# A recurrence's products with x in half-blocks of four steps with a fixed order, and the first chunk's gates moved into its head

## The chip, the core and the metric

One core of a Trainium2 chip runs the whole program. The metric is the time of one execution in device microseconds, given as the median of several runs; a profile is one execution. The engines are named as in the profile: PE (TensorE; PEld are its weight loads), DVE (VectorE), ACT (ScalarE), POOL (GpSimd), SP (SyncE, which here issues most DMAs). They run side by side, each works its own queue in order, and they wait for each other by semaphores.

## What is computed

Input x is 64 sequences of 64 steps of 256 numbers (4096 tokens), cond is 64 x 256. The program is a chain of two layers with residual sums. Each has a conditioning, an attention-like part, a second conditioning and a feed-forward part. Two pieces of layer 1 matter here:

```python
# conditioning: a plain recurrence; h starts from cond
xW = x @ Wx + b
h[t] = tanh(h[t-1] @ Wh + xW[:, t])            # Wh, Wx: 256 x 256

# "attention": a state-space block on h, inner width 512, 16 states
xi, z = split(h @ W_in)                        # 512 and 512
xc = silu(conv4(xi) + b_conv)                  # causal, 4 taps
delta_lr, B, C = split(xc @ W_xproj)           # 16, 16, 16
delta = softplus(delta_lr @ W_dt + b_dt)
s[t] = exp(delta * A) * s[t-1] + delta * B * xc
y = (sum over states of s * C + D * xc) * silu(z) @ W_out
```

Around them stand, in order of time: a conditioned scan and attention, a quantized feed-forward part (layer 0), then these two, then two mixtures of experts.

## The kernel before

All of it is float32 unless a line says otherwise. Feature rows lie on the 128 partitions, so 256 features are two halves, k = 0 and 1 (or o = 0 and 1 on the output side); tokens lie along the free axis. A framework schedules the instructions of each engine from the program text: it keeps data dependences, gives each a semaphore wait, and may move instructions past each other. An *issue order token* on an instruction pins its place among the instructions with the same token.

**Recurrence** (`rnn`, lines 711 to 756). PSUM tiles of 8 steps x 64 sequences hold what goes into tanh, one bank for each output half: tag `ps` for o = 0, tag `acc` for o = 1, four buffers each. Such a pair is a block; there are eight. First the products with x, xW, are put into the block (`ahead`, line 718): 8 "pieces" of 256 columns each, a piece being 32 sequences x 8 steps for one o and one k. Then, for each step, four products with Wh (line 745; two k, two o, 64 columns each) are added, and two tanh on ACT (line 754) write the new state into `hs`. A step needs the tanh of the step before. After each step one piece of the *next* block is asked for (line 755). Order is up to the scheduler, which can move pieces ahead of where they stand in the text.

In the profile every fp32 product shows as two weight loads and two matmuls.

**State-space stage** (`mamba`, lines 787 to 1052). The 4096 tokens are cut into 8 chunks of 512. `head(c, v)` (line 834) makes a chunk's inputs: four products with W_in (line 844, two matrix products each), which ACT (line 848) and DVE (line 851, three instructions) turn into the convolution; one Silu over the 512 rows (line 855); the product with W_xproj (line 859); softplus in pieces on PE, ACT, DVE and POOL (lines 883 to 897). `gates(c, v, i0)` (line 900) makes silu(z) for half of the rows: two products with W_in (line 906), two copies (line 909), a Silu (line 912). Both are generators that yield after each piece, so that they can be spread over a loop.

The loop (line 995) runs 32 steps a chunk, 256 in all. A step takes two scans on DVE (line 1009) and one product with C (line 1011), with the decay exp(delta A) from ACT (line 977), delta B xc from POOL (line 970), C spread over partitions by PE (line 922, tile `cb`), and eight transposes on PE that sum over the states (line 1025). The next chunk's head and this chunk's gates are queued in `pieces` (line 1001) and taken at a fixed rate, 40 for 30 steps (line 1041); what is left is run two steps before the chunk's end (line 1013).

Chunk 0 has no loop before it, so its head runs alone, ahead of the loop (line 984). Its gates are the first entries of `pieces`. Exp and Silu need different tables on ACT, and a change of table is a load (`ACT_TABLE_LOAD`).

PSUM tiles for single products come from `one()`, which in the first head goes round four tags (line 813) and afterwards always takes `mp` (line 986).

## Time and profile before

| | us |
|---|---|
| median of 10 runs | 2877.03 (2873.50 to 2880.23) |
| the profiled execution | 2877.23 |
| its span, first to last instruction | 2875.2 |
| recurrence, first Wh product to last tanh | 638.8 to 738.3 |
| head of chunk 0, to the first scan | 738.3 to 786.5 |
| chunk 0 of the state loop, nearly | 786.5 to 905 |

The page gives shares of the span in which each engine is busy: PE 84%, DVE 61%, ACT 49%, POOL 45%. They are means over stages with different limits and say little about one stage. The mean granted clock of TensorE is 0.917 of full speed. How to read the rows that follow: a timeline row has the start and duration in us, the engine, the line of the kernel, the operation, the tile it writes `<-` the tiles it reads, the shape and how many instructions are merged; `[1.31 <-ACT dA L977]` says that the engine stood idle for 1.31 us before it and which instruction ended that.

### The profile page before, as it was taken

To read this page: it belongs to the slowest core of one execution; us is meant where nothing else is said; L and a number is where in the kernel's file an instruction comes from. 1 tells how busy PE (TensorE), PEld (TensorE's weight loads), DVE (VectorE), ACT (ScalarE), POOL (GpSimd) and SP (SyncE) were. 2 spreads that over 40 slices of the span, in tenths; PEclk is the share of its full clock that TensorE was granted. 3 is DMA by queue.
4 is the path that set the end of the run, shared out by engine and by line. 5 is a ranking of instruction groups with operands and counts; after the bars stand their busy time and mean duration, and the time that the engine had idled before them with its cause. 6 is when DMAs were issued, how large, how long until landed. Compare 5 with 4: busy or idle time off the path is not lost.

```text
span 2875.2 us, 34770 instructions
## 1 busy us (share of the span) xinstructions
PE 2406.7 (84%) x12148; PEld 1701.0 (59%) x12148; DVE 1754.0 (61%) x2955; ACT 1412.6 (49%) x2406; POOL 1305.8 (45%) x1117
## 2 busy tenths in 40 slices
PE   4989977779666878888787888868987899999995
PEld 4633334458334555555455555556875778888885
DVE  0567648870299989898987888894244443323322
ACT  0567557764556676767475757643333222222220
POOL 0023335440178676767477777773745351111110
PEclk9979987889576989999899999989999999999998
DMA  9999700010121212121212121222686856555555
GB/s 237 370 358 341 231 25 19 19 63 5 33 71 67 79 64 71 59 82 56 70 63 92 63 96 67 90 80 89 223 288 228 313 192 251 221 187 205 210 189 183
DMA packets 183076, 406.06 MB, mean 141 GB/s; under 512 B 25312, under 2 KB 89056, under 8 KB 177520
## 3 DMA queue, kind: packets, MB, share of 16 engines
q1 hardware_dynamic: 169456, 366.80, 38.0%
q0 software_dynamic: 13440, 36.98, 3.3%
q8 instruction: 98, 1.61, 0.2%
q14 instruction: 82, 0.67, 0.1%
HBM read 280.76 MB, written 144.98 MB: 148 GB/s over the span
## 4 chain that ended last, share of the span: by engine, by line
PE 44%; DVE 20%; ACT 9%; issue 7%; POOL 4%; DMA 3%; SPq 0%; DVEq 0%; POOLq 0%; ACTq 0%
DVE hb L1009 12%; PE ps L1603 11%; PE acc L1501 8%; DVE hb L1011 3%; PE yp L1025 2%; PE ps L1570 2%; PE mq L1739 2%; PE mp L906 2%; PE mq L1755 2%; DVE xc L851 1%; PE ps L628 1%; PE ps L745 1%; POOL hb L970 1%; PE acc L745 1%; PE ps L1611 1%
## 5 line engine op out<-in xcount | busy, mean ns | idle before, releaser
L970 POOL TENSOR_TENSOR hb<-dx,Bn 128x1024 f32<-128x1024 f32 x256 | 601.1, 2358 | 259.0 <-PE yp L1025 252.6
L1009 DVE TENSOR_TENSOR_SCAN hb<-dA,hb 128x512 f32<-128x512 f32 x512 | 603.0, 1209 | 34.6 <-ACT dA L977 32.1
L977 ACT ACTIVATE dA<-delta,A 128x504 f32<-128x504 f32 x512 | 344.5, 683 | 309.3 <-DVE hb L1009 306.7
L1025 PEld LDWEIGHTS yp<-ident,hb 128*128 128x128 f32 x2048 | 267.1, 151 | 184.2 <-issue 146.1
L1011 DVE TENSOR_TENSOR hb<-hb,cb 128x1024 f32<-128x1024 f32 x256 | 312.2, 1220 | 79.2 <-PE cb L922 61.9
L1603 PE MATMUL ps<-gxT,w 128*128 128x256 f32 (+1 forms) x1600 | 323.7, 361 | 0.8 <-DVE gxT L1478 0.8
L1603 PEld LDWEIGHTS ps<-gxT,w 128*128 128x128 f32 x1600 | 276.5, 190 | 46.1 <-issue 11.6
L1025 PE MATMUL yp<-ident,hb 128*128 128x128 f32 x2048 | 301.5, 291 | 0.0
L1739 PE MATMUL mq<-x,moe_s 128*128 128x256 f32 x896 | 251.5, 413 | 48.3 <-ACT up L1746 26.8
L1277 POOL DMA_INDIRECT ffn_y<-gy,to x72 | 69.2, 961 | 432.2 <-ACT gy L1503 420.0
L1739 PEld LDWEIGHTS mq<-x,moe_s 128*128 128x128 f32 x896 | 170.0, 205 | 113.7 <-ACT up L1746 35.8
L1607 DVE TENSOR_TENSOR gh<-gs,ps 128x256 f32<-128x256 f32 (+1 forms) x200 | 78.7, 394 | 207.8 <-ACT gs L1606 207.6
L922 PE MATMUL cb<-parts,pick 80*128 80x512 bf16 x256 | 105.0, 410 | 115.3 <-DVE hb L1011 100.2
L1501 PE MATMUL acc<-w,gh 128*128 128x256 f32 (+1 forms) x864 | 187.4, 387 | 0.0
L1606 ACT ACTIVATE gs<-ps 128x256 f32<-128x256 f32 (+1 forms) x200 | 72.4, 362 | 231.3 <-PE ps L1603 225.4
L1503 ACT ACTIVATE gy<-acc,wt 128x256 f32<-128x256 f32 x152 | 67.0, 472 | 239.3 <-PE acc L1501 231.5
L1501 PEld LDWEIGHTS acc<-w,gh 128*128 128x128 f32 (+1 forms) x864 | 145.7, 189 | 30.6 <-issue 13.8
L426 POOL TENSOR_TENSOR E<-E,z 128x1024 f32<-128x1024 f32 x32 | 61.6, 1925 | 199.4 <-DVE z L425 121.6
L1755 PE MATMUL mq<-moe_s,sh 128*128 128x256 f32 x448 | 115.4, 396 | 6.2 <-ACT up L1746 6.2
L444 PE MATMUL out<-oT,M 128*128 128x512 f32 x256 | 117.9, 604 | 1.5 <-ACT oT L437 1.5
L1277 POOL DMA_INDIRECT moe_y<-gy,to x80 | 78.3, 978 | 79.9 <-ACT gy L1503 54.0
L1755 PEld LDWEIGHTS mq<-moe_s,sh 128*128 128x128 f32 x448 | 83.1, 195 | 41.9 <-issue 20.3
(462 smaller groups left out, 4463.7 us busy)
## 6 DMA issues: line engine op xcount, KB each, us to landing
w<-ffn_w SPq DMA_DIRECT2D x40, 2176.0 KB, 9.3
Bn<-B SPq DMA_DIRECT2D x128, 512.0 KB, 3.6
moe_x<-fill SPq DMA_DIRECT2D x130, 260.0 KB, 5.8
ffn_x<-fill SPq DMA_DIRECT2D x129, 260.0 KB, 6.0
w<-moe_w SPq DMA_DIRECT2D x48, 512.0 KB, 4.5
ffn_w<-in_ffn_W_dram SPq DMA_DIRECT2D x16, 640.0 KB, 8.5
gx<-moe_x SPq DMA_DIRECT2D x32, 260.0 KB, 4.9
gx<-ffn_x SPq DMA_DIRECT2D x32, 260.0 KB, 9.3
```

The lines of the kernel that those rows point to most:

```text
L444: nc.tensor.matmul(ps, M[:, o, ts(k, P)], v.o[:, o], start=(o == 0), stop=(o == H // 2 - 1))
L922: nc.tensor.matmul(t, pick[:, n : n + 1].to_broadcast([rows, P]), v.parts, start=True, stop=True)
L970: nc.gpsimd.tensor_mul(hb, vs[c].dx[p], Bn[:, n % NB, :].unsqueeze(1).to_broadcast([P, PI, CH]))
L977: nc.scalar.activation(decays[s][i][:, :, 1:], seq(vs[c].delta[p][:, i, :])[:, :, 1:], AF.Exp, scale=w.A[:, p * PI + i, n : n + 1],)
L1009: ins = nc.vector.tensor_tensor_scan(h, dA[i].rearrange("p b l -> p (b l)"), h, 0.0, ALU.mult, ALU.add)
L1011: ins = nc.vector.tensor_tensor(hb, hb, cb.unsqueeze(1).to_broadcast([P, PI, CH]), ALU.mult)
L1025: nc.tensor.matmul(yp[i][:, t, :], hb[:, i, ts(t, P)], g.ident, start=(n == 0 and t == 0), stop=(n == S - 1 and t == CH // P - 1), is_tran ...
L1277: i = self.g.nc.gpsimd.indirect_dma_start(out=self.y, out_offset=bass.IndirectOffsetOnAxis(ap=to, axis=0), in_=y, in_offset=None)
L1501: nc.tensor.matmul(po[s], h, w, start=(i == 0), stop=(i == n - 1))
L1603: nc.tensor.matmul(ps[:, j, :], v.w12[:, k, ts(j * (full + 1) + i, P)], v.xT[:, k, :], start=(k == 0), stop=(k == KD - 1))
L1739: nc.tensor.matmul(ps[:, i % 2, :], w[:, k, ts(i, P)], xu[:, k, :], start=(k == 0), stop=(k == KD - 1))
L1755: nc.tensor.matmul(ps[:, t, :], h[:, i, ts(t, P)], self.s2[:, i, :], start=(i == 0), stop=(i == NS - 1))
```

## The change

In the recurrence a piece is now all 64 sequences x 4 steps (still 256 columns), and the outer loop of `ahead` is over the two halves of a block, four steps each. Four pieces are made ahead of step 0. From then on one piece is made after each step, for the four steps that begin up to four steps later: in steps 4 to 7 of a block the first half of the next block, in steps 0 to 3 the second half of the same block. The pieces and the Wh products carry one order token, so they stay in the order of the text. Nothing changes in the number and size of the products, the tanh or the tiles.

In the state-space stage, `gates(0, vs[0], 0)`, the first half of chunk 0's gates, runs inside chunk 0's head after the four convolutions and ahead of the Silu. It is dropped from the loop's `pieces` for chunk 0 alone. So the pieces behind it come four places sooner in that chunk.

```diff
+    TG = TB // 2
+    order = lambda ins: g.tc.stamp_issue_order_token(ins.ins, "recurrence")
     def ahead(t0, ps):
-        for o in range(KD):
-            for half in range(2):
+        for half in range(2):
+            for o in range(KD):
                 for k in range(KD):
-                    nc.tensor.matmul(
-                        ps[o].rearrange("p t b -> p b t")[:, ts(half, B // 2), :],
+                    ins = nc.tensor.matmul(
+                        ps[o].rearrange("p t b -> p b t")[:, :, ts(half, TG)],
                         w.Wx[:, k, ts(o, P)],
-                        xv[:, k, ts(half, B // 2), t0 : t0 + TB],
+                        xv[:, k, :, t0 + half * TG : t0 + (half + 1) * TG],
...
+                    order(ins)
                     yield
...
+    blocks = [[bank(g, (P, TB, B), tag=("ps", "acc")[o]) for o in range(KD)] for _ in range(2)]
+    pieces = ahead(0, blocks[0])
+    for _ in islice(pieces, KD * KD):
+        pass
+    for t in range(L):
+        now = blocks[t // TB]
+        if t % TB == TG and t + TG < L:
+            if t + TG >= 2 * TB:
+                blocks.append([bank(g, (P, TB, B), tag=("ps", "acc")[o]) for o in range(KD)])
+            pieces = ahead(t + TG, blocks[(t + TG) // TB])
...
+                order(ins)
+        for o in range(KD):
+            nc.scalar.activation(hs[:, o, :, t], now[o][:, t % TB, :], AF.Tanh, bias=w.b[:, o : o + 1])
+        next(pieces, None)
...
-        for _ in head(0, vs[0]):
+        first = head(0, vs[0])
+        for _ in islice(first, 2 * NI):
+            pass
+        for _ in gates(0, vs[0], 0):
+            pass
+        for _ in first:
             pass
...
-                pieces = chain(pieces, gates(c, now, 0), islice(ahead, 2 * NI + 1), gates(c, now, PI), ahead)
+                pieces = chain(pieces, gates(c, now, 0) if c else (), islice(ahead, 2 * NI + 1), gates(c, now, PI), ahead)
```

## The prediction

> **What bounds the kernel now.** I read the page's engine shares first, then the stretch tables with the granted clock for 600 to 920 us, where the recurrence and the head of the state-space stage lie, then the timeline there. As a whole the kernel is bound stage by stage, and nothing overlaps the recurrence: between 640 and 738 us only TensorE and ACT work. One step, in the timeline:

> ```profile
> 644.33 0.30 PEld L745 LDWEIGHTS ps<-hs,Wh 128*128 128x128 f32 x2 [0.19 <-ACT hs L754]
> 644.38 0.42 PE L745 MATMUL ps<-hs,Wh 128*128 128x64 f32 x2
> ...
> 645.23 0.30 PEld L723 LDWEIGHTS acc<-xT,Wx 128*128 128x128 f32 x2
> 645.30 0.37 ACT L754 ACTIVATE hs<-ps,rb 128x64 f32<-128x64 f32 x1 [0.78 <-PE ps L745]
> 645.31 0.63 PE L723 MATMUL acc<-xT,Wx 128*128 128x256 f32 x2
> 645.52 0.38 ACT L754 ACTIVATE hs<-acc,rb 128x64 f32<-128x64 f32 x1
> ```

> The loop is: Wh products start (644.33), 0.97 later tanh of ps, 0.37 long, 0.05 later the next Wh: 1.39 a step. The second tanh ends 0.23 after the first. The product with x (L723, "a piece") runs beside the tanh and costs nothing. The stretch table (columns: stretch, its length, busy time of PE, PEld, DVE, ACT, POOL, then granted clock) shows what happens when the pieces are used up, at 702.2, 19 steps before the end:

> ```profile
> 690.00:698.99 8.99, 8.99 (x66) 7.73 (x65) 0.00 (x0) 3.94 (x14) 0.00 (x0) 1.00 0.00 0
> ...
> 705.81:709.23 3.42, 2.95 (x23) 2.52 (x22) 0.00 (x0) 1.30 (x5) 0.00 (x0) 1.00 0.02 5
> 709.23:719.47 10.24, 9.87 (x41) 9.00 (x40) 0.00 (x0) 3.79 (x11) 0.00 (x0) 0.50 0.00 0
> ```

> From 709.23 the clock is half, and a step takes 2.03 instead of 1.39:

> ```profile
> 715.18 0.37 ACT L754 ACTIVATE hs<-ps,rb 128x64 f32<-128x64 f32 x1 [1.21 <-PE ps L745]
> ...
> 717.21 0.37 ACT L754 ACTIVATE hs<-ps,rb 128x64 f32<-128x64 f32 x1 [1.21 <-PE ps L745]
> ```

> Fourteen steps are slow: 14 x 0.64 = 9.0 us. The clock comes back at 743.36, so the head's first products (L844, 0.86 apart in place of 0.43) are slow too. Later, in chunk 0 of the state loop, VectorE is the bound (111.5 busy of 118.5 us, 786.5 to 905), and the gates' Silu makes it wait, since ACT loads a table before and after it:

> ```profile
> 800.79 1.22 DVE L1009 TENSOR_TENSOR_SCAN hb<-dA,hb 128x512 f32<-128x512 f32 x1
> 803.32 1.22 DVE L1009 TENSOR_TENSOR_SCAN hb<-dA,hb 128x512 f32<-128x512 f32 x1 [1.31 <-ACT dA L977]
> ```

> **Part 1, the recurrence.** The work is the same: 64 pieces of 256 columns, 256 Wh products. What moves:

> (a) Start. Before, 8 pieces of the first blocks sit in the feed-forward stage, and 4 stand between step 0 and 1. The pieces taken out of that stage free nothing: ACT's copy at 614.02 waits for TensorE and its own queue alike (L658 ends at 613.98), and the last xT still lands at 637.15. Four pieces follow in both kernels, so step 0 starts at 638.83 in both.

> (b) The new wait. In the changed program's order on TensorE, listed with its waits, a piece of steps 0 to 3 of each block of 8 waits for ACT and the first Wh product behind it carries no wait: the piece writes the second half of the bank whose first half tanh is reading, so it starts only after tanh of its bank. Behind it in the queue stand the Wh products of the next step, and tanh waits for those. Two of the four pieces write ps, two acc. In steps 4 to 7 the piece goes to the other block's bank and stays beside tanh: 1.39.
> Price of a waiting piece: four pieces between 637.21 and the Wh product at 639.04 are 1.83, four between 639.88 and 641.66 are 1.78: 0.445 each, 0.05 more after a pause. From that Wh product to tanh are 0.81 to 0.86 (639.04 to 639.85, 641.66 to 642.52). So a ps step is 0.05 + 0.49 + 0.83 + 0.37 = 1.74, an acc step 0.23 more, 1.97. Bounds: 1.72/1.94 (no pause cost) and 1.83/2.06 (0.44 put on top of 1.39).
> (c) Sum: 16 x 1.74 + 16 x 1.97 + 31 x 1.39 = 102.4 us from step 0 to step 63, against 97.0 (638.83 to 735.85): **+5.4** (bounds +4.6 and +8.2). It holds the 9.0 won and 0.9 won at step 0.
> (d) End. Pieces now reach step 59. The last step at full speed takes 1.6 to the head's first product, at half 2.45: **-0.8**. But without pieces steps 60 to 63 are some 6 us long; before, the halving came 6.4 us after the last piece's end (702.84 to 709.23). So the clock may halve around step 63 (0 to +1.3 us), and the head starts at half clock again: I give no gain there, +0.3 for the steps.

> Will the clock hold in steps 0 to 3? Its changes stand on a grid of 3.41 us (709.23, 743.36, 750.19, 760.43, 763.84). I added up, for each grid stretch, the share in which columns were streamed (0.83 ns a column and pass pair, from L844's 512 columns 0.43 apart; weighted by rows used). Of 677 stretches at full clock, the 58 that were followed by half had shares up to 0.36 (one 0.39), those that were not, 0.365 and more (two lower); back to full it goes from about 0.73. A regular step has (8 x 0.053 + 2 x 0.21)/1.39 = 0.61, one without a piece 0.31, the waiting steps 0.49 and 0.43, and the worst stretch of 3.41 (Wh, pause, piece, Wh, pause, around steps 2 and 3) 0.36. So it should just hold.

> [...]

> **Part 2, gates inside the head.** Added to the head: four L906 products (0.86 each at full clock), two copies (0.58), one Silu (1.06); the table it needs is the one that xc's Silu loads anyway. TensorE is free there (from 747.93 to 755.10). In ACT's queue the copies, the load (1.28) and this Silu stand ahead of xc's Silu, which sets the head. Before, that began 14.84 after the first L844 (738.30 to 753.14). After: 12 products = 10.3 at full clock, some 1.9 for the slow start, then 0.2 + 0.58 + 1.28 + 1.06 = 15.3: **+0.5** (bounds -0.5 and +1.5 by how long the slow start is). What is behind (Wxp product, softplus, POOL's four 2.35 up to the first scan) keeps its length; one convolution of chunk 1 (L848, 0.78 on ACT; three L851) now stands in the gap before the first scan, where VectorE waited 2.22 for POOL.
> Removed from chunk 0's loop: the 1.31 above, and three L851 (0.65 each behind a scan, 805.78 to 806.44): **-3.3**. Bounds: -1.5 (only half of it, if another wait follows) and -9 (all idle of VectorE in chunk 0 is 9.2, some of it waits for cb behind half-clock products). The B store of chunk 1 passes one Bn load on SP; a Bn lands in 3.6 us and is asked for two steps ahead, so nothing; if not, one load, 3.6.

> **Sum**, on the profiled execution's 2877.23 (span 2875.2; the median of the ten, 2877.03, is the same): +5.4 - 0.8 + 0.3 + 0.5 - 3.3 = +2.1: **2879 us**, no change that can be told.

> **The rivals.**
> A, forecast: clock holds, 2873 to 2885. Chance 0.58.
> B, **slower: the clock halves within the recurrence.** Place: the pauses of 0.4 and 0.65 in steps 2 and 3. It decides at a share of about 0.36; mine is 0.36, and with acc steps of 2.06 it would be 0.33. At half clock a step with a piece is TensorE-bound, 4 x 0.42 + 0.86 = 2.54, share 0.67, below the 0.73 that brings the clock back, so it stays. A block then costs 4 x 1.15 + 2 x 1.18 + 2 x 1.37 = 9.7 more. From the middle on, 39 us: 2918; from the first block 78; only in the last, 2888. Against it: 0.42 to 0.45 in other stages held. 0.27.
> C, **faster by the loop**: VectorE's 9.2 us of waiting in chunk 0 go with the gates: 2879 - 8 = 2871. For: cb waits of 0.99 and 1.28 behind half-clock products. Against: L844 and the other gates remain. 0.10.
> D, the wait of (b) doesn't bite: 16 x 0.35 + 16 x 0.58 = 14.9 less: 2864. Against: the queue is in order. 0.05.

> **How the numbers follow.** 0.2% (5.8 us) is about what can be told from no change. Same: 0.42 of A, 0.05 of C: 0.47. Slower: 0.12 of A, all of B: 0.39. Faster: 0.04 of A, half of C, D: 0.14. The range leaves out most of C and D and B's early half: 2872 to 2915; A's own is 2873 to 2885.

> **What would show it.** Right: tanh-to-tanh spacing in a block 1.74, 1.74, 1.97, 1.97, then four of 1.39; granted clock 1.00 up to step 60; the step without piece gone but for the last four; xc's Silu directly behind the gates' Silu; no table load at the fifth scan. Wrong: clock 0.50 inside the recurrence (B), waiting pieces that start with tanh (D), or chunk 0 shorter by more than 5 us (C).

## The result and the profile after

| | kernel before | changed kernel |
|---|---|---|
| median, same chip | 2876.66 us (28 runs, 2870.25 to 2880.38) | 2890.55 us (8 runs, 2887.12 to 2897.12) |
| ratio, 95% interval | | 1.0052 [1.0043, 1.0061] |
| profiled execution, its span | 2877.23, 2875.2 | 2891.60, 2889.4 |

The change makes the kernel 0.5% slower. The forecast was 2879 with a range of 2872 to 2915. The time lies inside that range, but outside forecast A's own 2873 to 2885, and what happened is rival B. By stages of the two profiled spans:

| stage | before | after | difference |
|---|---|---|---|
| up to the first tanh | 639.9 | 640.8 | +0.9 |
| recurrence, first tanh to end of the last | 98.4 | 127.2 | **+28.8** |
| head of chunk 0, to the first scan | 48.2 | 46.8 | -1.4 |
| chunk 0 of the state loop | 131.1 | 124.5 | **-6.6** |
| chunks 1 to 7, to the last scan | 1034.3 | 1027.9 | -6.4 |
| mixtures, to the end | 923.3 | 922.2 | -1.1 |
| span | 2875.2 | 2889.4 | +14.2 |

**The waiting steps.** The timeline of the changed kernel, block 0, where the prediction showed the step of 1.39 us (L757 is tanh, L726 the piece, L752 the Wh products):

```profile
642.60 0.37 ACT L757 ACTIVATE hs<-ps,rb 128x64 f32<-128x64 f32 x1 [1.23 <-PE ps L752]
...
644.42 0.37 ACT L757 ACTIVATE hs<-ps,rb 128x64 f32<-128x64 f32 x1 [1.23 <-PE ps L752]
644.64 0.37 ACT L757 ACTIVATE hs<-acc,rb 128x64 f32<-128x64 f32 x1
...
645.06 0.70 PE L726 MATMUL acc<-xT,Wx 128*128 128x256 f32 x2 [0.46 <-ACT hs L757]
...
645.59 0.38 PE L752 MATMUL ps<-hs,Wh 128*128 128x64 f32 x2
...
646.45 0.37 ACT L757 ACTIVATE hs<-ps,rb 128x64 f32<-128x64 f32 x1 [1.45 <-PE ps L752]
...
648.49 0.37 ACT L757 ACTIVATE hs<-ps,rb 128x64 f32<-128x64 f32 x1 [1.45 <-PE ps L752]
...
649.88 0.37 ACT L757 ACTIVATE hs<-ps,rb 128x64 f32<-128x64 f32 x1 [0.79 <-PE ps L752]
```

Follow one acc step. The tanh of acc ends at 644.64 + 0.37 = 645.01. Only then, at 645.06, does the piece for acc start, and the bracket names tanh as what it waited for. The next Wh product stands behind it in the queue and starts at 645.59, though both halves of the state that it reads were written by then; the next tanh starts at 646.45. The spacing of the first tanh of each step in this block is 1.82, 1.82, 2.04, 2.04, then 1.39 four times. The step without a wait is the last row: 649.88 - 648.49 = 1.39.

**The clock.** The stretch table of the changed kernel (columns as before; the granted clock is the third figure from the end):

```profile
640.80:713.67 72.87, 64.54 (x433) 55.30 (x433) 0.00 (x0) 26.21 (x88) 0.00 (x0) 1.00 0.12 42
713.67:768.00 54.33, 51.89 (x198) 46.45 (x197) 0.70 (x4) 14.84 (x40) 1.10 (x5) 0.50 0.00 1
...
706.84:710.26 3.42, 2.95 (x21) 2.49 (x20) 0.00 (x0) 1.18 (x4) 0.00 (x0) 1.00 0.00 0
710.26:713.67 3.41, 2.49 (x18) 2.08 (x17) 0.00 (x0) 1.18 (x4) 0.00 (x0) 1.00 0.00 0
713.67:717.08 3.41, 3.41 (x14) 3.06 (x14) 0.00 (x0) 0.73 (x2) 0.00 (x0) 0.50 0.00 0
```

Full clock for 72.87 us, then half of it from step 3 of block 5 to the last tanh at 768.00. The stretch ahead of the fall, 710.26 to 713.67, holds the pauses of steps 2 and 3: TensorE is busy 2.49 of 3.41, less than in the other stretches. By the prediction's sum of columns its share is 0.367, the lowest of the recurrence up to there. (How the columns are placed within a row of the profile moves a share by up to 0.03; this stretch stays the lowest.) At half clock the shares are 0.50 to 0.70 as long as pieces last, below the 0.73 from which, by the prediction's count, the clock comes back, and it stays at half. At half clock a step with a piece beside tanh takes 2.56:

```profile
718.24 0.37 ACT L757 ACTIVATE hs<-ps,rb 128x64 f32<-128x64 f32 x1 [1.77 <-PE ps L752]
...
720.80 0.37 ACT L757 ACTIVATE hs<-ps,rb 128x64 f32<-128x64 f32 x1 [1.77 <-PE ps L752]
```

**Head and chunk 0.** ACT in the head of the changed kernel: the gates' copies, the table load, their Silu (L914), and directly behind it xc's Silu (L857) with no load of its own.

```profile
778.74 0.58 ACT L911 COPY sz<-mp 128x512 f32<-128x512 f32 x1 [0.94 <-PE mp L908]
780.45 0.59 ACT L911 COPY sz<-mp 128x512 f32<-128x512 f32 x1 [1.13 <-PE mp L908]
781.05 1.28 ACT L914 ACT_TABLE_LOAD   x1
782.35 1.06 ACT L914 ACTIVATE sz<-sz 128x1024 f32<-128x1024 f32 x1
783.31 1.89 ACT L857 ACTIVATE xc<-xc 128x2048 f32<-128x2048 f32 x1
```

It starts 15.3 us after the head's first product (768.05), 14.84 before. In chunk 0, VectorE's waits (releaser, total us, times, longest), first of the kernel before, 786.5 to 917.6, then of the changed one, 814.8 to 939.3:

```profile
DVE hb L1011 <- PE cb L922: 3.1, 4, 1.3
DVE hb L1009 <- POOL hb L970: 2.2, 1, 2.2
DVE hb L1009 <- ACT dA L977: 1.3, 1, 1.3
DVE hb L1011 <- DVE hb L1009: 0.5, 1, 0.5
```

```profile
DVE hb L1017 <- POOL hb L972: 2.2, 1, 2.2
DVE hb L1019 <- PE cb L924: 0.3, 1, 0.3
```

Not only the wait for ACT at the fifth scan is gone (1.3) but also 2.8 of the 3.1 for `cb` and the 0.5. With three convolution instructions fewer in this chunk (L851 x12, 8.59 us; L853 x9, 6.46 us, so 2.1) that makes 6.7, against 6.6 won.

### The profile page after: what moved, and what is told of

It is laid out like the page before. It is cut to its first block, busy times and chain, and to the rows that moved or that the text cites. A ratio compares the mean times of both kernels' runs of the same rounds, so it can differ in the third digit from the quotient of the medians.

```text
span 2889.4 us, 34770 instructions
## 1 busy us (share of the span) xinstructions
PE 2426.6 (84%) x12148; PEld 1721.1 (60%) x12148; DVE 1757.6 (61%) x2955; ACT 1410.2 (49%) x2404; POOL 1305.8 (45%) x1117
## 4 chain that ended last, share of the span: by engine, by line
PE 43%; DVE 20%; ACT 9%; issue 8%; POOL 5%; DMA 3%; SPq 0%; DVEq 0%; POOLq 0%; ACTq 0%
DVE hb L1017 12%; PE ps L1611 11%; PE acc L1509 8%; DVE hb L1019 3%; PE yp L1033 2%; PE ps L1578 2%; PE mq L1747 1%; PE mq L1763 1%; PE ps L628 1%; DVE xc L853 1%; PE ps L752 1%; PE mp L908 1%; POOL hb L972 1%; PE acc L752 1%; PE ps L1619 1%
```

## The experiments

They were run in three sets of four, each on one chip with its own runs of the kernel before. On the chips of the first two sets the kernel before takes 2936.75 and 2937.49 us; in their profiles the stages from the last scan to the end take 977 to 992 us in place of some 923. So only ratios and lengths of stages are compared across sets. **The theory** after the result: the change makes two separate costs, a wait for the bank that tanh reads (some +17 us), and through its pauses the fall of the clock (some +21 us), against what the spread pieces and the gates win. **Rivals**: the order or the shape of the pieces costs, not the bank; the clock falls for another reason than the missing columns; the gates in the head are part of the loss.

**1. The two parts apart.** `part1_only` has the recurrence's part of the diff alone, `part2_only` the state-space stage's part alone.

```diff
# part1_only: the state-space stage as before
-        first = head(0, vs[0])
...
+        for _ in head(0, vs[0]):
...
# part2_only: the recurrence as before, and
+        for _ in gates(0, vs[0], 0):
+            pass
...
+                pieces = chain(pieces, gates(c, now, 0) if c else (), islice(ahead, 2 * NI + 1), gates(c, now, PI), ahead)
```

> The recurrence of the changed kernel, with the head and the loop of the kernel before. Theory (the loss is all in the recurrence: half-bank pieces wait for tanh, the thinner load lets the clock halve; the gates in the head win 6 to 9 us afterwards): steps of 1.82 and 2.03 us in each first half-block, the clock halved somewhere in the recurrence, 2898 us (2890 to 2920). Rival (the gates in the head win nothing, and what was regained behind the recurrence is the clock alone): the same time as the changed kernel, 2890.

Measured: 2962.04 us, ratio 1.0076 [1.0048, 1.0105]. Recurrence 127.2 us, as in the changed kernel; the clock falls 72.9 us behind the first tanh, as there (713.67 - 640.8 and 714.09 - 641.2). Chunk 0 takes 131.3.

> The recurrence of the kernel before, with the gates of chunk 0 in its head. Theory: the first scan 0 to 1 us later against the recurrence's end, chunk 0 of the loop 5 to 7 us shorter, 2870 us (2867 to 2873). Rival (the regained time has nothing to do with the gates): 2877, chunk 0 as before.

Measured: 2926.12 us, ratio 0.9969 [0.9952, 0.9986]. Recurrence 98.4, head 47.9, chunk 0 124.4, with VectorE's waits there as in the changed kernel (2.2 and 0.3). So all the loss is in the recurrence, and part 2 by itself is a gain of 0.3%. The two ratios multiply to 1.0045, near the whole change's 1.0052.

**2. The wait taken away by banks.** `fresh_banks` keeps pieces, order and part 2, but each half-block of four steps has a bank pair of its own, so no piece writes a bank that tanh is reading.

```diff
-        if t % TB == TG and t + TG < L:
...
+        if t % TG == 0:
+            now = after
+            pieces = iter(())
+            if t + TG < L:
+                after = banks_()
+                pieces = ahead(t + TG, after)
...
-            nc.scalar.activation(hs[:, o, :, t], now[o][:, t % TB, :], AF.Tanh, bias=w.b[:, o : o + 1])
+            nc.scalar.activation(hs[:, o, :, t], now[o][:, t % TG, :], AF.Tanh, bias=w.b[:, o : o + 1])
```

> As the changed kernel, but each half-block of four steps has a bank of its own for each output half, so that no piece goes to a bank that tanh reads; one piece a step still, order still set. Theory (the wait comes from the shared bank, and the clock falls only because of it): tanh spaced 1.39 us in all steps, clock 1.00 until after the last piece, recurrence 89 us in place of 98 before, 2860 us (2855 to 2866). Rival (the fixed order itself, or the 64 x 4 shape of the pieces, makes the steps long): first half-blocks still 1.8 to 2.0 us a step, 2880 or more.

Measured: 2911.49 us, ratio 0.9904 [0.9886, 0.9923]; on another chip (`fresh_again`) 0.9920 [0.9896, 0.9943].

> The kernel with a bank pair of its own for each half-block of four steps, once more, beside the next one. Expected as measured: 88 to 89 us for the recurrence, the clock halved for some 7 us at its end, ratio 0.990 (0.988 to 0.993).

Recurrence 88.7 us in both. The timeline of `fresh_banks` shows two steps with a piece for ps and one with a piece for acc, 1.38 to 1.39 apart; the piece for acc (L722) starts beside tanh instead of behind it. Its stretch table shows the clock:

```profile
701.75 0.37 ACT L753 ACTIVATE hs<-ps,rb 128x64 f32<-128x64 f32 x1 [0.78 <-PE ps L748]
...
703.14 0.37 ACT L753 ACTIVATE hs<-ps,rb 128x64 f32<-128x64 f32 x1 [0.79 <-PE ps L748]
...
704.53 0.37 ACT L753 ACTIVATE hs<-ps,rb 128x64 f32<-128x64 f32 x1 [0.78 <-PE ps L748]
704.54 0.63 PE L722 MATMUL acc<-xT,Wx 128*128 128x256 f32 x2
...
705.91 0.37 ACT L753 ACTIVATE hs<-ps,rb 128x64 f32<-128x64 f32 x1 [0.78 <-PE ps L748]
```

```profile
635.20:721.75 86.55, 86.08 (x623) 74.43 (x623) 0.69 (x4) 37.96 (x126) 1.12 (x6) 1.00 0.10 35
721.75:728.58 6.83, 6.37 (x14) 3.60 (x15) 0.10 (x3) 1.54 (x4) 0.00 (x0) 0.50 0.47 154
```

One edit takes both costs away: no wait, hence no pause, and the clock falls only in the last steps, which have no piece. The bank decides, not order or shape. The price of the wait is 0.43 us in a ps step and 0.65 in an acc step (1.82 and 2.04 against 1.39).

**3. The wait kept, the pause filled.** To part the two costs, one more product of 192 columns is put behind the Wh products in steps 0 to 3 of each block, into a bank that nobody reads. First with columns 256 bytes apart, then (`after_filled_dense`) with columns side by side.

```diff
+        if t % TB < TG and t < L - TG:
+            if t % TB == 0:
+                spare = bank(g, (P, TB, B), tag="ps")
+            order(nc.tensor.matmul(spare[:, 0:3, :], w.Wx[:, 0, ts(0, P)], COLUMNS, start=True, stop=True))
# COLUMNS in after_filled:       xv[:, 0, :, 0:3].rearrange("p b t -> p t b")
# COLUMNS in after_filled_dense: g.xT[:, 0, 0 : 3 * B]
```

> As the changed kernel, but in steps 0 to 3 of each block one product of 192 columns into an unread bank is put behind the Wh products, where TensorE would wait for tanh. The wait stays. Theory (the share of streamed columns decides the clock): the share rises from 0.47 and 0.42 to 0.64 and 0.58, the clock stays at 1.00 through the recurrence, the steps stay 1.82 and 2.03, the recurrence is some 22 us shorter than in the changed kernel, 2869 us (2864 to 2877). Rival (the clock falls for another reason): it halves as before, 2888 or more.

Measured: 2932.61 us, ratio 0.9985 [0.9972, 0.9999]. Recurrence 109.2 us; the clock holds for 107 us behind the first tanh. But the ps steps take 1.97 where the changed kernel has 1.82: the filler is itself late.

> The changed kernel with one product of 192 consecutive columns into a bank that nobody reads in steps 0 to 3 of each block, behind the Wh products: as the first such run, but without the stride. The waits stay, the columns of the pause are filled. Theory (two separate costs, wait and clock): the clock holds to about step 60, the waiting steps take 1.82 and 2.04 as in the changed kernel's first blocks, and the recurrence takes 105 to 107 us (127.2 changed, 98.3 before). With 6.6 us won in chunk 0, ratio 0.998 to 1.001. Rival (the filler is in the way whatever it reads): spacings of 1.95 to 2.05 again, 109 us, ratio 0.9985 or more, which the spacings alone tell apart.

Measured: 2871.46 us, ratio 0.9984 [0.9973, 0.9996]. Timeline and stretch table:

```profile
637.06 0.37 ACT L761 ACTIVATE hs<-ps,rb 128x64 f32<-128x64 f32 x1 [1.23 <-PE ps L752]
...
638.89 0.37 ACT L761 ACTIVATE hs<-ps,rb 128x64 f32<-128x64 f32 x1 [1.23 <-PE ps L752]
...
640.94 0.37 ACT L761 ACTIVATE hs<-ps,rb 128x64 f32<-128x64 f32 x1 [1.46 <-PE ps L752]
...
643.00 0.37 ACT L761 ACTIVATE hs<-ps,rb 128x64 f32<-128x64 f32 x1 [1.46 <-PE ps L752]
...
644.39 0.37 ACT L761 ACTIVATE hs<-ps,rb 128x64 f32<-128x64 f32 x1 [0.78 <-PE ps L752]
```

```profile
635.20:738.84 103.64, 101.21 (x684) 86.08 (x684) 0.69 (x4) 37.16 (x124) 1.14 (x6) 1.00 0.08 30
738.84:745.66 6.82, 6.33 (x17) 3.88 (x17) 0.10 (x3) 1.50 (x4) 0.00 (x0) 0.50 0.39 120
```

The steps are those of the changed kernel's first blocks (1.83, 1.83, 2.05, 2.05, 1.39), the clock is full for 103.64 us, and the recurrence takes 106.65. This parts the sum: 88.01 (no wait, full clock; `fresh_tail_dense` in 5) + **18.64 by the waits** + **20.57 by the clock** = 127.22. By the spacings the waits are 16 x 0.43 + 16 x 0.65 = 17.3 of the 18.64; most of the rest is the last step of this run, at half clock again (2.02). By the two ratios to the kernel before (0.9984 and 1.0052) work that nobody needs makes the changed kernel 0.7% faster, because it keeps the clock up.

**4. The kernel before, in fixed order and filled.** `before_ordered` only adds the order token to the old pieces (8 steps x 32 sequences) and the Wh products. `before_filled` adds a token on the Wh products and a 256-column filler from step 44 on; `ordered_tail` is `before_ordered` with a filler of consecutive columns in the last 8 steps.

```diff
# before_ordered
+    order = lambda ins: g.tc.stamp_issue_order_token(ins.ins, "recurrence")
...
+                    order(ins)          # pieces
...
+                    order(ins)          # Wh products
# before_filled: no token on the pieces, and behind the Wh products
+            if t >= 44:
+                if t % TB == 4:
+                    spare = bank(g, (P, TB, B), tag="ps")
+                order(nc.tensor.matmul(spare[:, 0:4, :], w.Wx[:, 0, ts(0, P)], xv[:, 0, :, 0:4].rearrange("p b t -> p t b"), start=True, stop=True))
# ordered_tail: before_ordered, and
+            if t0 + TB == L:
+                if t == t0:
+                    spare = bank(g, (P, TB, B), tag="ps")
+                order(nc.tensor.matmul(spare[:, 0:4, :], w.Wx[:, 0, ts(0, P)], g.xT[:, 0, 0 : 4 * B], start=True, stop=True))
```

> The kernel before, with an order token on the Wh products and, in steps 44 to 63, one more product of 256 columns into a bank that nobody reads, behind the Wh products of the step. It takes no wait out and puts none in; it only gives TensorE columns to stream where the pieces have run out. If the clock follows the share of streamed columns, the granted clock stays at 1.0 through the recurrence, the 14 steps of 2.03 us take 1.39, and the recurrence takes 87 to 90 us in place of 98.3: 9 to 12 us less than the kernel before, ratio 0.996 to 0.997. If the slow steps come from something else (the pieces' absence itself, the end of the tiles, ACT), the steps stay at 2.03 and the ratio is 0.999 to 1.002.

Measured: 2945.34 us, ratio 1.0026 [1.0011, 1.0041], against both expectations. The clock falls at 702.94, when the first filler has just started (702.75). Without tokens of their own the pieces had been pulled further ahead; the last of a row stands at 697.21, and the stretch from 699.53 has no piece and no filler, with a share of 0.35. The fillers came one stretch too late, and then made the slow steps longer (2.56 in place of 2.03 at half clock, 1.77 at full). The run does not test what it was meant to. It shows the way back, though:

```profile
702.94:716.60 13.66, 13.66 (x53) 12.30 (x53) 0.00 (x0) 3.81 (x12) 0.00 (x0) 0.50 0.00 1
716.60:720.00 3.40, 3.40 (x17) 2.39 (x17) 0.00 (x0) 0.90 (x3) 0.00 (x0) 1.00 0.00 0
...
730.00:743.00 13.00, 13.00 (x75) 9.55 (x73) 0.00 (x0) 4.69 (x16) 0.00 (x0) 1.00 0.00 1
```

In the stretch up to 716.60, with fillers and a piece, the share is 0.75 by the prediction's sum; the clock is full from there to beyond the last tanh, with shares of 0.47 to 0.63. In the kernel before, without fillers, it stayed at half to the end of the recurrence.

> The kernel before with one order token on its pieces (still 32 sequences x 8 steps) and its Wh products, and nothing else. All 8 pieces of the first block then stand ahead of step 0, and each later piece goes behind its step into the bank pair of the next block, which no tanh reads yet. My theory, that the cost in the changed kernel is the shared bank and not the order: no step waits, all have 1.39 us as long as the clock holds, the pieces last to step 55, the clock halves some 3 to 7 us behind that, and 4 to 6 steps of 2.03 are left in place of 14. Recurrence 90 to 94 us from first to last tanh (98.3 before), ratio 0.997 to 0.999. Rival: the fixed order itself stretches the steps, as in the changed kernel; then spacings of 1.8 to 2.0 appear in half of the steps, and the ratio is 1.002 or more.

Measured: 2930.27 us, ratio 0.9968 [0.9954, 0.9983]. All steps 1.37 to 1.40 up to the 59th, four of 2.0 at the end, recurrence 90.7 us. Its stretch table:

```profile
642.50:717.93 75.43, 75.43 (x545) 65.31 (x544) 0.00 (x0) 33.18 (x110) 0.00 (x0) 1.00 0.10 37
...
721.34:724.76 3.42, 2.73 (x20) 2.21 (x19) 0.34 (x3) 1.61 (x6) 0.00 (x0) 1.00 0.00 0
724.76:733.20 8.44, 7.95 (x32) 7.19 (x32) 0.00 (x0) 3.20 (x9) 0.00 (x0) 0.50 0.01 2
```

The fixed order costs nothing by itself; it wins 7.7 us (98.4 to 90.7): ten slow steps fewer are 10 x 0.64 = 6.4, and 1.3 is the gap of 2.67 behind step 0, whose four pieces now stand ahead of it.

> The kernel before with the order token on pieces and Wh products and, in the last 8 steps, which have no piece left, one more product of 256 columns into a bank that nobody reads. It reads its columns side by side in memory (256 consecutive tokens of x), not 256 bytes apart as in the fillers so far, whose two passes took 1.05 us in place of 0.62. If the clock follows the share of streamed columns, and if it was the stride that stretched the earlier fillers' steps to 1.77 us, all 63 spacings are 1.37 to 1.40, the clock stays at 1.0 to the last tanh, and the recurrence takes 88 to 89 us, 9 to 10 less than before; ratio 0.996 to 0.997. If a product that nobody needs stretches a step whatever it reads, the last 8 steps take 1.6 to 1.8; if the clock falls for another reason than the missing columns, they take over 2.0, as in the kernel without filler.

Measured: 2860.06 us, ratio 0.9928 [0.9908, 0.9948]. The stretch from the first tanh to the last:

```profile
641.00:729.13 88.13, 88.13 (x635) 76.14 (x635) 0.00 (x0) 38.66 (x128) 0.00 (x0) 1.00 0.10 36
```

All 63 spacings are 1.37 to 1.40, the clock is full to 740.32, beyond the last tanh at 729.1, and the recurrence takes 88.1 us. This is the clean test that `before_filled` was not: with columns streamed, the slow steps go. The whole time is lower than the expected ratio of 0.996 to 0.997. Against the kernel before on the same chip (6) the span is 18.3 us shorter: 10.3 in the recurrence, 3.6 in the head, but also 6.8 in chunks 1 to 7, where the programs are the same; these 6.8 are not explained.

**5. The end filled.** `fresh_tail` and `fresh_tail_dense` are `fresh_banks` with a filler of 256 columns in steps 60 to 63, 256 bytes apart and side by side.

```diff
+        if t >= L - TG:
+            if t == L - TG:
+                spare = bank(g, (P, CH // B, B), tag="ps")
+            order(nc.tensor.matmul(spare[:, 0:4, :], w.Wx[:, 0, ts(0, P)], COLUMNS, start=True, stop=True))
```

> The same, and in steps 60 to 63, which have no piece left, one more product of 256 columns each into a bank that nobody reads. If the clock follows the share of streamed columns, it stays at 1.0 up to the last tanh, the last steps take 1.39 and the head begins at full clock: 1 to 4 us less than with fresh banks alone, ratio to the kernel before 0.989 to 0.990. Rival: the clock only falls one stretch later, in the gap between the last tanh and the head's own products, and the head loses what the recurrence wins: no difference of more than 1 us.

Measured: 2923.95 us, ratio 0.9954 [0.9939, 0.9969], so slower than `fresh_again` on the same chip, which neither expectation had. The clock is held to 744.12, but the last three spacings are 1.77. The timeline tells why; a piece, and then a filler of as many columns:

```profile
722.36 0.62 PE L722 MATMUL acc<-xT,Wx 128*128 128x256 f32 x2
...
723.74 1.05 PE L758 MATMUL ps<-xT,Wx 128*128 128x256 f32 x2
```

Both are two passes of 256 columns. The one that reads every column 256 bytes from the last takes 1.05 us in place of 0.62 and delays the next step. But this costs little: the recurrence takes 89.1 us, 0.5 more than in `fresh_again`. Of the 10.1 us between the two spans 4.1 lie ahead of the first tanh and 5.0 behind the last scan, where the kernels are the same; why is open.

> Bank pairs of their own for each half-block, with one product of 256 consecutive columns in steps 60 to 63 into a bank that nobody reads. If the stride was what cost in the first such run: 88 to 88.5 us for the recurrence, clock at 1.0 to the head, and no more than 1 us better than fresh banks alone, since the head's length does not follow the clock at its start (47.7 us with the clock held, 47.3 without): ratio 0.990 to 0.993. Rival: the last steps take 1.77 again and the ratio is 0.995.

Measured: 2856.92 us, ratio 0.9915 [0.9894, 0.9937], the lowest time. Recurrence 88.0 us at full clock throughout, all spacings 1.37 to 1.40:

```profile
640.60:728.60 88.00, 88.00 (x635) 76.02 (x635) 0.00 (x0) 38.62 (x128) 0.00 (x0) 1.00 0.10 35
```

The head takes 45.6 us, 2.7 less than before, and 44.7 in `ordered_tail`. Up to xc's Silu, the clock at its start is worth some 2 us, against the expectation: with part 2, the Silu starts 13.4 us behind the head's first product in the two kernels that begin the head at full clock (this one and `fresh_tail`), and 15.3 to 16.0 in the other six; without part 2 it is 12.5 (`ordered_tail` and `before_filled`) against 14.4 to 14.9. Behind the Silu the heads differ again: 31.4 us to the first scan here, 33.1 in `fresh_tail`, so the whole head alone did not show it. That this kernel beats `fresh_banks` can't be told, since the two intervals overlap.

**6. The kernel before once more.**

> The kernel before itself, for a profile of it on this chip, whose runs of it are some 60 us longer than those of the first chip. Recurrence 98.3 us with the clock's fall within one or two stretches of the same step (the 50th), head 48, chunk 0 131; the 60 us in the mixtures behind the state loop, which would then take about 980 us in place of 923. If the place of the stretches is random against the program, the fall moves by up to 2.5 steps; if the pieces' end decides alone, by less than that. Ratio 1.000.

Measured: 2877.74 us, ratio 0.9999 [0.9988, 1.0010]. This chip was not one of those with the long mixtures (923.4 us from the last scan to the end), so the 60 us stay unplaced but for the stages named above. Recurrence 98.4; the clock falls 69.4 us behind the first tanh, as in the first profile and in `part2_only` (69.4 each).

## Why the prediction was right and wrong

- **(a) Start**: right; the first tanh is 0.9 later, with a scatter of 635 to 642.5 us over the 14 profiles.
- **(b) The new wait**: right in mechanism and place, in four steps of each block, two by ps and two by acc. The size was low: 1.74 and 1.97 against 1.82 and 2.04, near the upper bounds of 1.83 and 2.06. The rows show the terms: from piece to Wh product 0.53, not 0.49 (645.06 to 645.59), and from there to tanh 0.86, not 0.83 (to 646.45). At full clock (c) would have been 16 x 1.82 + 16 x 2.04 + 31 x 1.39 = 104.9 us in place of 102.4: 2.5 more. (The upper bounds add up to +8.3, not +8.2.)
- **"So it should just hold" is the step that failed.** It took one worst stretch of 0.36, on the edge of the rule it had just read off, and let that stand as a pass. Two things spoke against that. The steps came out longer (2.04), which lowers the worst stretch to 0.35; the prediction has longer steps only under rival B, with 0.33 for steps of 2.06, where block 3 with such steps comes to 0.34. And, which it left out, the stretches move against the steps: a block takes 13.27 us, four stretches 13.65, so with each block they lie 0.38 us later. The lowest share in blocks 0 to 5 was 0.406, 0.436, 0.453, 0.451, 0.418, 0.367: the worst position came sooner or later, and in block 5 it did. Laid anywhere over the first five blocks, a stretch has below 0.37 in places about 0.3 us wide in each block, nearly as wide as the move. Rival B, at 0.27, was what happened, and it cost 20.6 us.
- **B's own numbers** held: steps of 2.56 at half clock (2.54), waiting steps of 2.86 and 3.28 (2.92 and 3.34), a block of 22.5 us in place of 13.3, so 9.2 more (9.7). Its +39 stood for a fall in the middle; the fall came at step 43 of 64, and 20.6 us were lost.
- **The pauses were short, and the grid held.** In the stretch ahead of the fall no pause of TensorE was longer than 0.46 us, two of these were enough, and filling them (3) kept the clock. In the kernel before, the longest wait of TensorE's products between 702 us and the fall at 709.23 was 0.24. The half clock of the changed kernel, 713.67 to 771.70, is 17 stretches of 3.41 us.
- **(d) End and the head**: -1.4 against -0.8 + 0.5. xc's Silu starts 15.3 us after the first product, as forecast; what is behind it took 1.9 less, which was put at unchanged. Half of that is the product with W_xproj: 5.3 us of it ran at half clock before (755.10 to 760.43), 3.4 after (785.35 to 788.76). The rest goes with a wait of ACT for TensorE, 1.01 us at 767.35 before, at half clock; the changed kernel, at full clock there, doesn't have it. So the forecast left out where the clock's falls lie in the head; heads of 44.7 to 48.3 us occur over the profiles.
- **Chunk 0**: -6.6 against -3.3, inside the bounds. The forecast counted the wait for ACT and the three convolutions; the waits for `cb`, 3.1 us, went too. That was rival C's mechanism, at 3.3 of the 8 us that it set beside the forecast, and by the prediction's sign (more than 5 us) C is seen here beside B. The 9.2 us of idle time that C goes by hold 2.22 ahead of the first scan; 7.0 lay in the stretch (118.5 - 111.5). Only part 2 does it: 131.3 with part 1 alone, 124.4 with part 2 alone.
- **Not foreseen**: -6.4 in chunks 1 to 7. The 14 profiles range from 1028 to 1039 us there, with and without part 2, so this is not put down to the change.
- From forecast to result, in the spans: +2.1, recurrence +23.1 (28.8 - 5.4 - 0.3), head and end -1.1, chunk 0 -3.3, the other stages -6.6: +14.2. The recurrence alone would have given 2902. That the time came out nearer to the forecast is in part luck: 6.6 us of it lie in stages where the two programs are the same. And the range held the time because it was drawn to take in most of B, not because the clock held.

## What to carry to other kernels

Work moved beside a serial chain must not write a bank that the chain's reader has open: ask for each moved product which bank it writes and who reads it then, because here the wait held up everything behind it in the queue (18.6 us, gone with a bank pair for each half). If a bound is a share over fixed stretches of time, don't test one position: slide the stretch over the whole pattern, and if the period is not a multiple of it, count on the worst one. And before a rewrite, try pinning the order alone: one token on the old products gave 0.3%, and with products to stream in its last 8 steps 0.7%, of which a little over half lies in the recurrence.
